# Layer 0 of a four-layer graph network: tie count, list sweeps and overflow rounds placed elsewhere between the two steps

## The chip, the cores and the metric

The kernel runs on one core of a Trainium2 chip. The metric is the device time of one execution in microseconds, the median of three runs. A profile of one more execution, recorded by the hardware, gives each instruction's start and duration. TensorE is called PE here, its weight loads PEld, VectorE DVE, ScalarE ACT, GpSimd POOL and SyncE SP. SP only issues transfers.

## The reference

There are 4096 nodes of 256 features and a sparse 4096 x 4096 adjacency matrix. Four layers follow each other, each as `x = x + layer(relu(layernorm(x)), adj)`. The change lies in layer 0, which takes two steps of a diffusion; its attention is cut to the largest probabilities that together reach 0.9:

```python
def _top_p_attention(X, W1, W2, W3):
    q = X @ W1.T @ W2.T
    k = X @ W3.T
    probs = softmax(q @ k.T)
    idx = argsort(-probs)
    sp = take_along_axis(probs, idx); cs = cumsum(sp)
    keep_sorted = cs - sp < 0.9
    A = probs * mask            # mask: keep_sorted put back in place
    return A / A.sum(-1, keepdims=True)

R = S + eye(N); R = R / R.sum(-1, keepdims=True)   # S: adj
Xf = Xa = X
for n in range(2):
    A = _top_p_attention(Xa, W1, W2, W3)
    Xf = R @ Xf
    Xa = A @ Xa
    Z = Z + Xf @ U1[n].T + Xa @ U2[n].T
return layernorm(X + Z) * ln_g + ln_b
```

Layers 1 to 3 are a graph convolution with tanh, a graph attention with four heads, and a convolution with relu. They stand after everything told here.

## The kernel before

The rows are worked in 32 blocks of 128 (`NB`), numbered 0 to 31. For each block, step n of layer 0 makes the row of logits (PE, `logits`, into PSUM pieces `pl`), its exponentials (ACT, `exps`, into a tile `e` of 128 x 4096), and looks for the threshold that keeps 0.9 of the sum. Nothing is sorted. The search is a ping-pong between two engines:

- ACT makes full or partial passes over `e`: `s0 r0` and `s1 r1` over 1024 columns, `s2 r2` and `s3` over all 4096 (a sign pass and a relu pass, line L1269). The number is the round.
- DVE turns their sums into the next guess by a dozen operations of one column each: `u0`, `u1`, `u2`, and at the end `bnd`, of some forty such operations.
- DVE then takes everything below the bound (`below`, L1475, a pass over 4096 columns into the tile `near`), the eight largest of each of 16 pieces (`seg`, L1483), merges them to a list of the largest (`lst`, L1495), decides the threshold (`dec`), and cuts the row (`cut`, L1535, another pass over 4096).

A row can have several values equal to the threshold. `ties_pe` (PE, L1558) counts such rows of a block by a product of one column, `ties` (ACT, L1564) copies the count to an integer, and `drop` (DVE, L1543) reads it into a register and branches: only if it isn't zero are the surplus equal values removed. Everything that reads the cut row comes after. In step 0 the count of a block is put into the last column of the PSUM bank in which the block before has its keys and queries (`keys_pe`, tag `pr`, one bank), so it must come after `keys_pe`.

After the cut, PE transposes the row in eight groups (`flip0` to `flip7`, L1604, into PSUM tiles of the tag `pmisc`, two banks), ACT copies each (`take`, L1610), and PE multiplies (`attend`, L1619). In step 0 the result is turned (`turn_pe`, `turn`, the copy `zt`), multiplied by weights (`xa_pe`, `h_pe`, copies `hu` by `copy_xa` and `store_h`, which go to the tables `heads_d`, `base_d`, `far_d`, `near_d`), and made to the keys and queries of step 1 (`keys_pe`, copied by `keys` as `kt` and `q`). The tag `pr` has one bank, so `keys_pe` waits until `hu` has been copied from it.

The order of PE, DVE and ACT is written out by hand. `ORDERS[n]` is a table of words, `name@offset`; `period(b)` goes through it and calls each word for block b + offset, so a period holds pieces of several blocks. A word is skipped if it was done ahead of its time. `LEADS[n]` is such a list before the first period of a step. In the last periods of step 0 (30 to 34) other pieces are put in by `inserts`: after the word named, the listed functions are called. They do three further things:

- `guessing(k)`: steps of `guess(1, ...)`, first estimates of the thresholds of step 1. For each of seven groups of 512 queries there is a product `py` (PE, L1040), a DVE operation (L1044) and four products (L1051), then a chain of 16 short DVE operations (L1063 to L1077). `last_queries` copies the queries of blocks 30 and 31 (ACT) into `near`, which the seventh group reads.
- `listing(k)`, and `L` in the lead: steps of `listed_columns`, which makes the lists of nonzero columns of the adjacency matrix. The step at `take1` of period 32 transposes `marks` (L787). 20 rounds of a MAX8 and a MATCH_REPLACE8 follow (L818, L819); the last three, the sweeps (`SWEEPS`), go over all 1024 keys. Then come a reduction (`fits`) and four copies of overflow lists by SP (L830), 8 overflow rounds of 32 rows (L840, L841), and two index tables, `column` and `adj_row`.
- `ahead1(b, words)`: words of step 1 for block b, done during step 0.

Step 1 mixes neighbours with the lists: POOL gathers rows by `column` and `adj_row` (L889, indirect DMAs, from `far_d` in the first half), PE multiplies them (L920, L921, tile `pr`). Each period of step 1 has two such mixes. POOL and SP are not under the written order: there the tile framework orders the instructions. [...] A PE product of float32 shows as two instructions in the profile.

Of the kernel before, what the change touches and what calls it, by code (L numbers as in the profile page):

```python
# [63 lines left out]
F32 = mybir.dt.float32  # L64
# [12 lines left out]
P = 128  # L77
N = 4096
D = 256
NB = N // P  # L80
# [585 lines left out]
def fast_layers(  # L666
# [85 lines left out]
    def marking(pool, marks):  # L752

        parts = []
        for k in range(NB * QUARTERS):
            while len(parts) < min(k + ADJ_BUFS, NB * QUARTERS):
                b, q = divmod(len(parts), QUARTERS)
                parts.append(pool.tile([P, CA, P], F32, name="adj"))
                nc.sync.dma_start(parts[-1], adjt[b, :, q * CA : (q + 1) * CA, :])
            b, q = divmod(k, QUARTERS)  # L760
            nc.vector.tensor_reduce(
                marks[:, :, q, b], parts[k], AX.X, ALU.max, apply_absolute_value=True
            )
            yield
# [165 lines left out]
    ps = layer0.enter_context(tc.tile_pool(name="ps", bufs=2, space=PSUM))  # L930
# [53 lines left out]
    def some(steps, k):  # L984

        for _ in zip(range(k), steps):
            pass
# [21 lines left out]
    def by_node(kt, r):  # L1009

        pt = ps.tile([P, 4, P], F32, name="pt", tag="pmisc")
        for k in range(4):
            nc.tensor.transpose(pt[:, k, :], kt[:, (4 * r + k) * P : (4 * r + k + 1) * P], ident)
        nc.scalar.copy(kn[:, :, :P], pt)

    def add_moments(r, pm, last):

        for k in range(4):
            nc.tensor.matmul(
                pm[:, : P + 1], kn[:, k, :P], kn[:, k, :], start=(r == 0 and k == 0), stop=(r == last and k == 3)  # L1020
            )
# [58 lines left out]
    def front(h0, kt, xs, marked, early):  # L1080
# [97 lines left out]
    G G M u2:0 s2:1 s3:0 M G G r2:1 logits0:2 exps0:2 M G G M bnd:0|u2:1  # L1178
    """,
        """  # L1180
    u2:0 logits1:1 s3:0 exps1:1 s0:1 r0:1 L4 bnd:0 below:0 L99 logits0:2 exps0:2 u0:1 s1:1 r1:1 logits1:2 exps1:2 u1:1 s2:1
    r2:1
    """,
    )

# [19 lines left out]
    def layer0_step(n, kt):  # L1205
# [344 lines left out]
        def ties_pe(b):  # L1550

            s = state[b]
            if n or b == 0:
                bank = ps1.tile([P, 512], F32, name="pties", tag="pr")
            else:
                bank = state[b - 1]["pkq_bank"]
            s["ties"] = bank[:1, 511:]
            nc.tensor.matmul(s["ties"], end["extra"][:, b : b + 1], ones, start=True, stop=True)  # L1558
# [472 lines left out]
    with ExitStack() as st:  # L2031
        s0 = st.enter_context(tc.tile_pool(name="s0", bufs=1))
        h0 = s0.tile([P, NB, D], F32, name="h0")
        kt0 = s0.tile([P, N // 2], F32, name="kt0")

        wu = []
        for i, u in enumerate((u1t, u2t)):
            wu.append(s0.tile([P, DC, 2, D], F32, name=f"wu{i}"))
            for n in range(2):
                nc.sync.dma_start(wu[i][:, :, 1 - n, :], u[n].rearrange("(c p) m -> p c m", p=P))  # L2040
        adj_pool = st.enter_context(tc.tile_pool(name="adj0", bufs=ADJ_BUFS))
        marked = marking(adj_pool, marks)
        period, verify, enter, early, lead, query = layer0_step(0, kt0)
        period1, verify1, enter1, early1, lead1, _ = layer0_step(1, kt1)

        def ahead(i, guesses):
            some(guesses, EARLY_GUESSES[i] if i < len(EARLY_GUESSES) else 0)
            for b, words in EARLY.get(i, ()):
                early(b, *words.split())

        with tc.tile_pool(name="front", bufs=1) as xs, tc.manual_schedule(engines=MANUAL):
            guesses = front(h0, kt0, xs, marked, ahead)
        own = st.enter_context(tc.tile_pool(name="own0", bufs=1))
        with tc.manual_schedule(engines=MANUAL):
            enter(h0, own, marked)
            lead(LEADS[0], M=marked, G=guesses)
            for b in range(NB - 2):
                period(b)
            some(marked, NB * QUARTERS)

            pm = ps.tile([P, 2, 512], F32, name="pl")
            first = adj_pool.tile([P, CA, P], F32, name="adj").rearrange("p l i -> p (l i)")[:, :512]
            nc.sync.dma_start(first, q_d[1][:, :512])
            lists = listed_columns(marks, e_pool.tile([P, N], F32, name="e"), ps)

            def sums_of(lo):
                if lo:
                    return ps1.tile([P, NB, 2], F32, name="pst", tag="pa")
                return pm[:, 1, : 2 * NB].rearrange("p (b k) -> p b k", k=2)

            guesses = guess(1, pm[:, 0], sums_of, first, SAMPLED[1] * P)

            def nodes(r):
                return lambda: by_node(kt1, r)

            def sums(r):
                return lambda: add_moments(r, pm[:, 0], SAMPLED[1] // 8 - 1)

            def listing(k):
                return lambda: some(lists, k)  # L2080

            def guessing(k):
                return lambda: some(guesses, k)

            def ahead1(b, words):
                return lambda: early1(b, *words.split())

            def queries():
                for g in range(4):
                    cols = slice(max(g * 1024, 512), min((g + 1) * 1024, (NB - 2) * P))  # L2090
                    nc.sync.dma_start(near[:, cols], q_d[1][:, cols])

            def last_queries():
                for b in range(NB - 2, NB):
                    nc.scalar.copy(near[:, b * P : (b + 1) * P], query(b))

            period(
                NB - 2,
                inserts={
                    "take1": [nodes(0)],  # L2100
                    "take2": [sums(0)],
                    "take3": [nodes(1)],
                    "take4": [sums(1)],
                    "take5": [nodes(2)],
                    "flip7": [sums(2), guessing(1)],
                    "take7": [guessing(1)],
                    "attended": [guessing(1)],
                },
            )
            period(  # L2110
                NB - 1,
                inserts={
                    "take1": [guessing(1)],
                    "attend7": [guessing(1), ahead1(0, "logits0")],
                    "turn": [ahead1(0, "exps0")],
                },
            )
            queries()
            period(
                NB,  # L2120
                inserts={
                    "take1": [listing(1), ahead1(0, "logits2 exps2")],
                    "take2": [listing(2), ahead1(0, "s0")],
                    "take3": [listing(3), ahead1(0, "r0")],
                    "take4": [listing(3), ahead1(0, "u0"), ahead1(1, "logits0")],
                    "take5": [listing(3), ahead1(0, "s1 r1")],
                    "take6": [listing(3)],
                    "take7": [listing(3), ahead1(0, "u1")],
                    "turn": [ahead1(1, "exps0 logits2 exps2")],
                },  # L2130
            )
            period(
                NB + 1,
                inserts={
                    "keys": [ahead1(0, "logits1 exps1 s2 r2"), guessing(3), listing(1)],
                    "xa_pe": [guessing(2), listing(1)],
                    "copy_xa": [last_queries],
                    "h_pe": [guessing(9), listing(2)],
                },
            )  # L2140
            period(NB + 2)
            lead1(LEADS[1], L=lists)
            verify()

    with ExitStack() as st:
        s1 = st.enter_context(tc.tile_pool(name="s1", bufs=1))
# [125 lines left out]
    with ExitStack() as st:  # L2272
# [3 lines left out]
        ps = st.enter_context(tc.tile_pool(name="gcnps", bufs=2, space=PSUM))  # L2276
# [76 lines left out]
    with ExitStack() as st:  # L2353
# [4 lines left out]
        ps = st.enter_context(tc.tile_pool(name="gatps", bufs=2, space=PSUM))  # L2358
# [153 lines left out]
    with ExitStack() as st:  # L2512
        adj_pool = st.enter_context(tc.tile_pool(name="lastadj", bufs=6))
        wk = st.enter_context(tc.tile_pool(name="lastwk", bufs=3))
        ps = st.enter_context(tc.tile_pool(name="lastps", bufs=2, space=PSUM))
# [15 lines left out]
@with_exitstack  # L2531
def graph_layers(ctx: ExitStack, tc: tile.TileContext, *given: bass.AP):
    nc = tc.nc
    dram = ctx.enter_context(tc.tile_pool(name="verdict", bufs=1, space=DRAM))
    wrong = dram.tile([1, 1], I32, name="wrong")
    fast_layers(tc, *given, wrong)
    again = nc.values_load(wrong[0:1, 0:1], min_val=0, max_val=2 * N + 2 * P)
    with tc.If(again != 0):
        general_layers(tc, *given)
# [54 lines left out]
```

## Time and profile before

| | |
|---|---|
| median of 3 runs | 2910.83 us (2905.03 to 2912.14) |
| the profiled execution | 2910.45 us, its span 2908.7 us |
| PE, DVE, ACT, POOL busy | 87%, 80%, 68%, 38% of the span |
| ACT full and partial passes (L1269), 320 in all | 859.5 us |
| step 1, 1200 to 1300 us: PE, DVE, ACT, POOL busy | 94.62, 88.65, 82.71, 66.55 us |

The page divides the span into 40 slices of 72.7 us, one digit for each, the busy share in tenths. A row of an engine's timeline gives start, duration (both in us), engine, line, operation, output and input, how often, and in brackets how long the engine had been idle before it and what ended that. A row "DVEq L1543" is the branch of `drop`. Step 0 ends and step 1 begins between about 1050 and 1190 us.

### The profile page before, as it was taken

To read this page: it belongs to the slowest core of one execution; us is meant where nothing else is said; L and a number is where in the kernel's file an instruction comes from. 1 tells how busy PE (TensorE), PEld (TensorE's weight loads), DVE (VectorE), ACT (ScalarE), POOL (GpSimd) and SP (SyncE) were. 2 spreads that over 40 slices of the span, in tenths; PEclk is the share of its full clock that TensorE was granted. 3 is DMA by queue.
4 is the path that set the end of the run, shared out by engine and by line. 5 is a ranking of instruction groups with operands and counts; after the bars stand their busy time and mean duration, and the time that the engine had idled before them with its cause. 6 is when DMAs were issued, how large, how long until landed. Compare 5 with 4: busy or idle time off the path is not lost. (4 is left out here: it accounts for less than half of the span.)

```text
span 2908.7 us, 43850 instructions
## 1 busy us (share of the span) xinstructions
PE 2523.0 (87%) x12359; PEld 1850.5 (64%) x12359; DVE 2312.7 (80%) x9516; ACT 1976.6 (68%) x3289; POOL 1098.0 (38%) x1152
## 2 busy tenths in 40 slices
PE   5769999999999884699999999999895776999777
PEld 4537777777777762467676766677773554788444
DVE  4799999999999866898989879999964765888200
ACT  2689999999999634887888878788520123999100
POOL 3200000000000001488888554344425752764476
PEclk7779999999999996899999999999996887999887
DMA  7611222222222113244444433334337653654576
GB/s 254 222 55 59 92 69 87 89 69 91 80 75 89 40 40 103 64 126 126 122 136 118 134 111 102 99 117 123 101 98 227 209 165 104 173 164 121 160 210 183
DMA packets 227371, 349.57 MB, mean 120 GB/s; under 512 B 34727, under 2 KB 160172, under 8 KB 227116
## 3 DMA queue, kind: packets, MB, share of 16 engines
q1 hardware_dynamic: 185820, 237.70, 25.7%
q0 software_dynamic: 40320, 108.72, 13.6%
q8 instruction: 101, 1.65, 0.2%
q14 instruction: 154, 1.26, 0.1%
q10 hardware_dynamic: 976, 0.23, 0.0%
HBM read 280.22 MB, written 66.28 MB: 119 GB/s over the span
## 5 line engine op out<-in xcount | busy, mean ns | idle before, releaser
L1269 ACT ACTIVATE unread<-e,next_pair 128x4096 uint8<-128x4096 f32 (+1 forms) x320 | 859.5, 2686 | 160.9 <-DVE next_pair L1365 109.0
L1619 PE MATMUL pa<-va,at 128*128 128x256 f32 x2048 | 495.2, 387 | 0.0
L1619 PE MATMUL pa<-h,at 128*128 128x256 f32 x2048 | 469.0, 379 | 0.1
L1619 PEld LDWEIGHTS pa<-va,at 128*128 128x128 f32 x2048 | 376.4, 193 | 65.4 <-issue 21.6
L1619 PEld LDWEIGHTS pa<-h,at 128*128 128x128 f32 x2048 | 376.6, 190 | 45.3 <-issue 0.5
L1483 DVE MAX8 best<-near 128x8 f32<-128x256 f32 x1024 | 394.6, 415 | 0.1
L1610 ACT COPY at<-pat 128x512 f32<-128x512 f32 x512 | 284.0, 577 | 135.3 <-PE pat L1604 135.1
L1236 PE MATMUL pl<-kt,qb 64*128 64x512 f32 x1024 | 280.4, 657 | 91.3 <-ACT e L1250 88.4
L1604 PE MATMUL pat<-ident,e 128*128 128x128 f32 x2048 | 305.0, 279 | 51.2 <-DVEq L1543 25.1
L1604 PEld LDWEIGHTS pat<-ident,e 128*128 128x128 f32 x2048 | 240.0, 142 | 139.1 <-DVEq L1543 47.8
L1485 POOL COPY eighth<-best 128x16 f32<-128x16 f32 x64 | 47.1, 736 | 722.7 <-DVE best L1483 711.7
L1250 ACT ACTIVATE e<-pl,minus_guess 128x1024 f32<-128x1024 f32 x256 | 284.3, 1125 | 26.8 <-PE pl L1236 26.7
L1475 DVE SCALAR_TENSOR_TENSOR near<-e,end_hi 128x4096 f32<-128x4096 f32 x64 | 286.6, 4477 | 0.1
L1535 DVE SCALAR_TENSOR_TENSOR e<-e,end_t 128x4096 f32<-128x4096 f32 x64 | 286.2, 4472 | 0.2 <-issue 0.2
L889 POOL DMA_INDIRECT vg<-v_d,column x256 | 243.4, 951 | 91.0 <-issue 67.7
L920 PE MATMUL acc<-vg,ac 128*128 128x256 f32 x640 | 215.9, 489 | 66.3 <-DMA vg<-v_d,column 29.6
L920 PEld LDWEIGHTS acc<-vg,ac 128*128 128x128 f32 x640 | 146.9, 247 | 132.1 <-issue 59.8
L1236 PEld LDWEIGHTS pl<-kt,qb 64*128 64x128 f32 x1024 | 89.8, 194 | 195.7 <-ACT e L1250 156.4
L889 POOL DMA_INDIRECT vg<-mixed_d,column x128 | 180.5, 1410 | 57.6 <-issue 32.4
L2407 PE MATMUL acc<-u,tabg 128*65 128x128 f32 x1280 | 170.2, 280 | 13.5 <-DVE u L2397 13.5
L889 POOL DMA_INDIRECT vg<-far_d,column x128 | 166.6, 1301 | 39.0 <-issue 38.1
L2394 ACT ACTIVATE u<-targets,tabg 128x128 f32<-128x128 f32 x544 | 162.1, 389 | 10.0 <-DMA targets_x<-steep_d 10.0
(608 smaller groups left out, 4427.7 us busy)
## 6 DMA issues: line engine op xcount, KB each, us to landing
adj<-in_adjt SPq DMA_DIRECT2D x128, 512.0 KB
ac<-adjc_d SPq DMA_DIRECT2D x64, 320.0 KB
adjc_d<-ac SPq DMA_DIRECT2D x32, 320.0 KB
vg<-v_d SPq DMA_DIRECT2D x64, 128.0 KB
targets<-steep_d SPq DMA_DIRECT2D x32, 256.0 KB
ac<-adjc_d SPq DMA_DIRECT2D x32, 256.0 KB
table_d<-tab SPq DMA_DIRECT2D x32, 132.0 KB
tabg<-table_d SPq DMA_DIRECT2D x32, 132.0 KB
```

The costliest lines, as they stand in the source:

```text
L889: nc.gpsimd.indirect_dma_start(out, None, rows, bass.IndirectOffsetOnAxis(ap=index, axis=0))
L920: nc.tensor.matmul(acc, ac[:, k, :], v[:, k, :], start=(k == 0), stop=False)
L1236: nc.tensor.matmul(pl[:, r, :], s["qb"][rows], kt[rows, j * 512 : (j + 1) * 512], start=True, stop=True,)
L1250: nc.scalar.activation(s["e"][:, j * 1024 : (j + 1) * 1024], pl.rearrange("p r c -> p (r c)"), AF.Exp, bias=minus_guess[:, b : b + 1], acc ...
L1269: nc.scalar.activation(unread[:, :width], s["e"][:, :width], func, bias=s["at"], scale=-1.0, accum_out=s["signs"] if func == AF.Sign else ...
L1475: nc.vector.scalar_tensor_tensor(near, s["e"], end["hi"][:, b : b + 1], s["e"], op0=ALU.is_lt, op1=ALU.mult, accum_out=s["low"])
L1483: nc.vector.max(best[:, k, :], near[:, k * (N // SEG) : (k + 1) * (N // SEG)])
L1535: nc.vector.scalar_tensor_tensor(s["e"], s["e"], last, s["e"], op0=ALU.is_ge, op1=ALU.mult, accum_out=s["held"])
L1604: nc.tensor.transpose(pt[:, k, :], s["e"][:, c * P : (c + 1) * P], ident)
L1610: nc.scalar.copy(at, s["pt", g])
L1619: nc.tensor.matmul(s["pa"], s["at", g][:, k, :], va[:, c, :D], start=(c == 0), stop=(c == NB - 1))
L2407: nc.tensor.matmul(s["acc"][:, h, :], s["tab"][:, k, h * (DK + 1) : (h + 1) * (DK + 1)], s["u"][:, k, h, :], start=(k == 0), stop=False,)
```

## The change

It has three parts, all of them of place and order.

- The tie count of block 31 (`NB - 1`) gets a bank of the tag `pmisc`. `ties_pe` and `ties` are done at the end of period 31, after `turn`; `drop`, `flip0` and `flip1` follow `cut` at once in period 32, before `store_h` and `keys_pe`.
- The four steps of `listing` in period 33 (three sweeps, and what follows them up to the SP copies) move into period 32, after `attended` and after `turn`.
- `u2` and `s3` of block 0 of step 1 move from the lead into period 33, after `copy_xa` and ahead of `last_queries`. In the lead, the rest of the lists goes from ahead of `logits0:2` to behind `u1:1`, in two pieces: eight steps there, the rest after `r2:1`.

```diff
@@ LEADS[1]
-    u2:0 logits1:1 s3:0 exps1:1 s0:1 r0:1 L4 bnd:0 below:0 L99 logits0:2 exps0:2 u0:1 s1:1 r1:1 logits1:2 exps1:2 u1:1 s2:1
-    r2:1
+    logits1:1 exps1:1 s0:1 r0:1 logits0:2 exps0:2 bnd:0 u0:1 below:0 s1:1 r1:1 logits1:2 exps1:2 u1:1 L8 s2:1 r2:1 L9
@@ ties_pe
             if n or b == 0:
                 bank = ps1.tile([P, 512], F32, name="pties", tag="pr")
+            elif b == NB - 1:
+                bank = ps.tile([P, 512], F32, name="pties", tag="pmisc")
             else:
                 bank = state[b - 1]["pkq_bank"]
@@ the end of step 0
+            def ahead0(words):
+                return lambda: early(NB - 1, *words.split())
+
@@ period(NB - 1)
-                    "turn": [ahead1(0, "exps0")],
+                    "turn": [ahead0("ties_pe ties"), ahead1(0, "exps0")],
@@ period(NB)
+                    "cut": [ahead0("drop flip0 flip1")],
                     "take1": [listing(1), ahead1(0, "logits2 exps2")],
...
-                    "turn": [ahead1(1, "exps0 logits2 exps2")],
+                    "attended": [listing(2)],
+                    "turn": [ahead1(1, "exps0 logits2 exps2"), listing(2)],
@@ period(NB + 1)
-                    "keys": [ahead1(0, "logits1 exps1 s2 r2"), guessing(3), listing(1)],
-                    "xa_pe": [guessing(2), listing(1)],
-                    "copy_xa": [last_queries],
-                    "h_pe": [guessing(9), listing(2)],
+                    "keys": [ahead1(0, "logits1 exps1 s2 r2"), guessing(3)],
+                    "xa_pe": [guessing(2)],
+                    "copy_xa": [ahead1(0, "u2 s3"), last_queries],
+                    "h_pe": [guessing(9)],
```

In the engines' instruction orders the same instructions stand in both kernels. On SP the four copies L830 come ahead of the store of `far_d` for block 30 instead of among the loads of `va` (the operand of step 1's products, read from `heads_d`); on POOL one branch comes ahead of three iotas.

## The prediction

> **What bounds the kernel now.** I read the page's slices first, then the busy time by stage, then each engine's timeline over the seam between the two steps of layer 0, about 1050 to 1190 us. Both steps keep TensorE (PE) over 90% busy; the seam does not.
>
> ```profile
> PE   5769999999999884699999999999895776999777
> 1050.00:1090.00 40.00, 34.06 (x152) 24.10 (x150) 20.30 (x86) 16.06 (x31) 0.10 (x1) 0.87 0.05 15
> 1120.00:1160.00 40.00, 11.02 (x27) 3.83 (x27) 30.69 (x145) 17.37 (x21) 8.18 (x9) 0.54 0.43 130
> 1160.00:1190.00 30.00, 3.90 (x10) 1.22 (x10) 20.76 (x117) 25.76 (x28) 19.83 (x23) 0.52 0.32 81
> ```
>
> The columns after the length are PE, weight loads, VectorE (DVE), ScalarE (ACT), POOL, then clock, DMA share, GB/s. From 1120 to 1190 PE works 15 us of 70: it waits for the first blocks' threshold search, a ping-pong of DVE and ACT. That search is the path. Its stops:
>
> ```profile
> 1060.44 0.16 DVE L773 MEMSET marks<- 128x8 f32 x4 [10.31 <-DVEq L1543]
> 1100.15 1.61 DVE L1044 SCALAR_TENSOR_TENSOR near<-py,mean,near 128x512 f32<-128x512 f32 x2 [13.54 <-PE py L1040]
> 1119.19 1.22 DVE L818 MAX8 e<-e 128x8 f32<-128x1024 f32 x1
> ...
> 1126.15 3.71 ACT L1269 ACTIVATE unread<-e,next_pair 128x4096 uint8<-128x4096 f32 x1 [12.50 <-DVE next_pair L1365]
> ...
> 1137.74 4.48 DVE L1475 SCALAR_TENSOR_TENSOR near<-e,end_hi 128x4096 f32<-128x4096 f32 x1
> ...
> 1156.88 3.70 ACT L1269 ACTIVATE unread<-e,next_pair 128x4096 uint8<-128x4096 f32 x1
> ...
> 1145.93 0.60 PE L853 MATMUL pt<-e 32*128 32x16 f32 x2 [21.41 <-DVE e L848]
> ...
> 1190.78 1.10 PE L1604 MATMUL pat<-ident,e 128*128 128x128 f32 x8 [2.24 <-DVEq L1543]
> ```
>
> Block 31's cut ends at 1050.1 and its flips start at 1060.4, because its tie count stands behind keys_pe. DVE then has a 13.5 us hole, yet its last sweep of the lists comes after it and holds ACT's s3:0 for 12.5 us. Then L99 (8 us, 1142.15 to 1150.14) precedes u0:1, so block 1's full pass s2:1 starts at 1156.88. Step 1's first flip follows at 1190.78.
>
> **The change part by part.** Sums are against the profiled execution: 2910.45 us, span 2908.7 plus 1.75. The median, 2910.83, is 0.4 above.
>
> *Ties ahead.* ties_pe moves to just after turn_pe (ends 1053.19), ACT's tied copy (0.14) after zt (ends 1053.82). In the row above, flips start 1.0 us after the tied copy's end, so flip0 moves from 1060.4 to about 1054.9. Only part arrives. ACT's take0 remains queued behind hu, kt and q, and keys_pe stays tied to hu (1056.6), now behind eight transposes. Cold (keys 2.2 us as traced) take0 is at 1059.7 and the marks transposes at 1060.3, against 1062.2: gain 2.0. Warm (keys 1.2, marks 1.0, the next four logits 0.8 less) gain 4.9. The Trainium skill ("TensorE: Matmul & The Clock Gate", Part 1: The HAM clock gate) halves the clock after an idle window of about 3.4 us. The old gap (3.36 us) gave 0.50; the new gaps, 1.7 and 1.2, would by that rule stay warm: 4.9. But gaps of 1.17 and 1.61 before 1026.7 were followed by a granted 0.57 in 1028 to 1032, which argues for 2.0. I take 3. PE is 4.00 busy in every 4 us from 1064 to 1088, so this arrives whole at the end of period 32.
>
> *Sweeps into the hole.* Four listing steps move: three sweeps at 1.22+0.09+1.21 with small gaps, 2.56 each, and the tail (fits 1.22, memsets 0.35, 0.30, 0.33): 9.9 us. They now follow u1:0, from 1083.6 to 1093.5; the next DVE work waits for py at 1097.1. Cover 3.6 us, so cost 0; without it, up to 9.9. Of the old places, two lay under the PE work of xa_pe and h_pe (worth 0); the third plus tail (1119.19 to 1123.99) frees 4.8. The four list copies on SP (2.53 us of issue) move from the middle of the va loads to ahead of the far_d store of block 30, which they hold to about 1096. What queues behind (q_d, a qb, heads_d) is next wanted by logits0:2 at about 1120. Worth 0. On POOL only a branch passes three iotas.
>
> *u2:0 and s3:0 to copy_xa.* u2:0 (2.16 us, as from 1123.90) follows the sixth L1044, at 1108.1, ending 1110.3; s3:0 runs to 1114.2 instead of 1130.0. Its price: behind s3:0 on ACT stand the two query copies (0.5) that the seventh py needs, so py moves from 1112.8 to 1114.7 after a PE gap of 4.8 us. By the same rule that gap ends cold; the trace's cold rows are about twice the warm ones, so guess ends its products 1.0 (0 to 1.9) later still: 1118.6 against 1115.78, its chain of 3.5 at 1122.1 against 1119.3. The hu copy behind goes out at 1115, a far_d row first gathered after 1147: nothing.
>
> *Overflow rounds behind the first pass.* Now bnd:0 starts at 1122.1 (was 1131.5), 6.25 long: 1128.4; u0:1 2.0: 1130.4, its s0 and r0 done by 1124.3 since PE no longer stands at L852/L853; below:0 4.5: 1134.9 while s1 and r1 run; u1:1 2.0; s2:1 at 1137.0. That is 19.9 ahead of 1156.88.
>
> *Given back.* The rest of the lists now lies between u1:1 and the end of u2:1: 0.4, eight rounds 5.5, 2.2 to the table, 1.5 to column, then 5.0 woven with u2:1 and verify: u2:1 ends 1151.5, where its r2:1 would allow 1146.2. So s3:1 starts 1151.6 against 1167.08: **15.5 ahead**. From there DVE and ACT have the old order; flip0 of block 0 comes at about 1175.3.
>
> *Does it reach the end?* In step 1 PE is 94.6 of 100 busy, and the mixes come every 29.5 us with no wait ahead of them. The gathers are the danger: column comes only 1.9 us sooner, so 18 gathers at 1.25 end at 1170, and 29 at 1184. PE wants the first mix at 1201.4, so that slack falls from about 46 to 31 us.
>
> ```profile
> 1149.38 1.11 POOL L889 DMA_INDIRECT vgx<-far_d,column  x1 [52.40 <-DVE e L869]
> ...
> 1216.89 2.34 PE L920 MATMUL pr<-vg,ac 128*128 128x257 f32 x10
> ...
> 1362.32 4.47 DVE L1535 SCALAR_TENSOR_TENSOR e<-e,end_t 128x4096 f32<-128x4096 f32 x1
> ...
> 1363.33 4.28 POOL L889 DMA_INDIRECT vg<-far_d,column  x1 [0.30 <-issue]
> ```
>
> A gather that meets a DVE pass took 4.28 us, not 0.95. The first batch met none; now it meets cut(0) and below(1). The Trainium skill ("SBUF — State Buffer", SBUF: two separate sides) speaks against the change: whoever starts first holds the shared port for its whole instruction. By the trace two meetings cost 6.7 us, by the rule up to 9.0. Either way the 29 end by 1193, of which the last eleven serve mixes at 1231 and later. Cost 0 by both.
>
> Sum: +3 (ties) +16.9 (search) −4.4 (lists) = 15.5; 2910.45 − 15.5 = **2895**, as a median too. With 2.0 or 4.9 for the first term, cold or warm py, and 1 us of weaving, 12 to 20: 2890 to 2899.
>
> **Rivals.** *Gain mostly not passed on (a part at most):* s3:0 waiting longer, the DVE sweeps reaching past py, or the take0 queue eating the ties. For it: four engines in order, each re-timed. Against: 3.6 us of cover. Time 2899 to 2905.
>
> *It doesn't do what it says:* gathers set the first mixes, so PE starts early and waits there; only their 1.9 us remain: 2909. Against: 31 us of slack.
>
> *Slower, by one mechanism:* in step 1's first half POOL has no idle left. Its cycle starts at 30.8 us with two blocked gathers, has one of 34.2 at 1311 to 1346, then locks at 29.5, lagging the mixes by 10.6 (1375.26 against 1364.65). If the new phase left it at 34.2, it would lose 4.7 us a period against PE. The cycle begun at 1219.5 ends at 1249.4 and serves a mix at 1276.0, 26 us later; used up in six of sixteen periods, that leaves ten times 4.7 on PE, less 15.5: 2942. It decides above 31.1 us a cycle (29.5 plus 26 over 16). Against: the blocked time shrinks when POOL falls behind, as the lock shows, and the phase of the passes to the mixes is set by the unchanged order.
>
> **How the numbers follow.** This kernel's measurement can tell 0.3% (8.7 us) from no change; the line is 2902.1. Forecast (2890 to 2899) 0.66; more than that (to 2884) 0.05; partly lost (2899 to 2905) 0.14, of which 0.09 is still beyond 0.3%; no gain 0.07; slower 0.08. Faster 0.80, same 0.12, slower 0.08. The range 2886 to 2905 leaves out no gain, slower, and a little at the fast end.
>
> **What would show it.** Right: flip0 of block 31 near 1055; sweeps ended before py; s3:0 near 1110; s2:1 near 1137; s3:1 near 1151.6; first mix near 1201 with no wait; all later stages shifted alike. Wrong: marks still at 1062; py(7) past 1118; a DMA wait ahead of L920 in the first periods; a POOL cycle above 31.1 us.

## The result, and the profile after

The kernel after takes 2894.2 us (median of 4 runs, 2889.9 to 2895.7) against 2911.05 for the kernel before (4 runs). The ratio is 0.9944, with a 95% interval of 0.9926 to 0.9962. That is 16.8 us less, outside the 0.3% that the measurement can tell from no change. Predicted were 2895 and 15.5 us less. The profiled execution spans 2893.8 us.

Its page's slices of TensorE (PE), and the stages by window (length, then PE, weight loads, VectorE, ScalarE, GpSimd, clock, DMA share, GB/s):

```profile
PE   5769999999999895799999989999985776999777
1120.00:1160.00 40.00, 14.05 (x36) 5.38 (x36) 32.41 (x182) 26.80 (x32) 8.50 (x9) 0.54 0.38 116
1160.00:1190.00 30.00, 16.70 (x70) 10.81 (x71) 26.90 (x127) 25.01 (x29) 24.21 (x20) 0.69 0.26 66
```

PE does 30.8 us of work between 1120 and 1190 where it did 15, because step 1's attention now begins inside that stretch. The timeline of the kernel after has these stops (start, duration, instruction, and in brackets the idle time ahead and what ended it). The line numbers moved by one: L1269 is now L1268, and behind the tie count L1604 is now L1605.

```profile
1055.10 0.59 ACT L1641 COPY zt<-pt 128x512 f32<-128x512 f32 x1 [3.79 <-PE pt L1636]
...
1056.82 1.06 PE L1605 MATMUL pat<-ident,e 128*128 128x128 f32 x8 [1.63 <-ACT e L1249]
...
1061.17 1.97 PE L787 MATMUL pt<-ident,marks 128*128 128x128 f32 x8 [1.13 <-ACT at L1611]
...
1098.26 1.61 DVE L1044 SCALAR_TENSOR_TENSOR near<-py,mean,near 128x512 f32<-128x512 f32 x2 [2.32 <-PE py L1040]
...
1111.53 3.71 ACT L1268 ACTIVATE unread<-e,next_pair 128x4096 uint8<-128x4096 f32 x1 [4.98 <-DVE next_pair L1364]
...
1115.23 0.48 ACT L2099 COPY near<-q 128x128 f32<-128x128 f32 x2
...
1115.77 2.08 PE L1040 MATMUL py<-near,mk 128*128 128x512 f32 x2 [4.67 <-ACT near L2099]
...
1138.99 3.71 ACT L1268 ACTIVATE unread<-e,next_pair 128x4096 uint8<-128x4096 f32 x1 [1.59 <-DVE next_pair L1364]
...
1142.82 3.71 ACT L1268 ACTIVATE unread<-e,next_pair 128x4096 uint8<-128x4096 f32 x1
...
1151.45 3.71 ACT L1268 ACTIVATE unread<-e,next_pair 128x4096 uint8<-128x4096 f32 x1 [2.28 <-DVE skip L1280]
...
1160.23 3.71 ACT L1268 ACTIVATE unread<-e,next_pair 128x4096 uint8<-128x4096 f32 x1 [2.43 <-DVE steep L1348]
...
1175.14 2.99 PE L1605 MATMUL pat<-ident,e 128*128 128x128 f32 x12 [2.23 <-DVEq L1542]
```

They are the copy `zt` of block 31, its first flips (1056.82), the marks (1061.17), the first L1044 behind the sweeps (1098.26), s3:0 (1111.53), the two query copies behind it (1115.23), the seventh py (1115.77), s2:1 and r2:1 (1138.99, 1142.82), s3:1 (1151.45), the next block's first full pass (1160.23) and the first flip of step 1's block 0 (1175.14, before 1190.78).

Two executions are not in step when they reach this seam. The copy `zt` of block 31 starts at 1055.10 here and at 1053.23 before, and over all profiles of this document it lies between 1047.0 and 1055.1. The same transposes one block earlier (block 30) lie between 1017.5 and 1023.4; most of this difference was already there at 210 us. From there to block 31's transposes it takes 28.9, 30.6 or 32.3 us (30.6 and 32.3 in two profiles of the kernel after). So I measure each profile by **S**, the stretch from the start of that copy to block 0's first flip: 137.6 us before, 120.0 after. (The expectations below call this point the end of the copy; their figures for S, too, count from its start.) Three rows of the kernel before, for comparison, are its `zt`, its marks and its s3:1:

```profile
1053.23 0.59 ACT L1640 COPY zt<-pt 128x512 f32<-128x512 f32 x1 [3.79 <-PE pt L1635]
...
1062.21 1.97 PE L787 MATMUL pt<-ident,marks 128*128 128x128 f32 x8
...
1167.08 3.71 ACT L1269 ACTIVATE unread<-e,next_pair 128x4096 uint8<-128x4096 f32 x1
```

The seam is 17.5 us shorter, and the product at L1837 (L1836 before) that starts at 2107.18 before starts at 2090.01 after: nothing is lost again in step 1. (The two profiled executions end 14.9 us apart; the 2.3 us between are lost in the layers behind, for a reason that I did not follow.) "Aligned" below means less 1.87, the difference between the two starts of `zt`.

### The profile page after: what moved, and what is told of

Its sections match the earlier page's. It is cut to its first block, busy times and chain, and to the rows that moved or that the text cites. A ratio compares the mean times of both kernels' runs of the same rounds, so it can differ in the third digit from the quotient of the medians.

```text
span 2893.8 us, 43853 instructions
## 1 busy us (share of the span) xinstructions
PE 2529.9 (87%) x12359; PEld 1856.8 (64%) x12359; DVE 2311.4 (80%) x9516; ACT 1975.2 (68%) x3289; POOL 1104.3 (38%) x1152
## 5 line engine op out<-in xcount | busy, mean ns | idle before, releaser
L1268 ACT ACTIVATE unread<-e,next_pair 128x4096 uint8<-128x4096 f32 (+1 forms) x320 | 859.6, 2686 | 160.4 <-DVE next_pair L1364 109.0
L1605 PE MATMUL pat<-ident,e 128*128 128x128 f32 x2048 | 305.0, 279 | 51.1 <-DVEq L1542 23.6
L1605 PEld LDWEIGHTS pat<-ident,e 128*128 128x128 f32 x2048 | 239.9, 142 | 138.9 <-DVEq L1542 46.3
L1484 POOL COPY eighth<-best 128x16 f32<-128x16 f32 x64 | 30.1, 470 | 702.1 <-DVE best L1482 691.5
L1249 ACT ACTIVATE e<-pl,minus_guess 128x1024 f32<-128x1024 f32 x256 | 284.1, 1124 | 17.7 <-PE pl L1235 17.5
```

Source lines behind the costliest of these rows:

```text
L1249: nc.scalar.activation(s["e"][:, j * 1024 : (j + 1) * 1024], pl.rearrange("p r c -> p (r c)"), AF.Exp, bias=minus_guess[:, b : b + 1], acc ...
L1268: nc.scalar.activation(unread[:, :width], s["e"][:, :width], func, bias=s["at"], scale=-1.0, accum_out=s["signs"] if func == AF.Sign else ...
L1605: nc.tensor.transpose(pt[:, k, :], s["e"][:, c * P : (c + 1) * P], ident)
```

## The experiments

All ratios are to runs of the kernel before on the same chip. The ratio is the estimate from all runs of a kernel, so it need not be exactly the quotient of the two medians. S comes from one profile each. The runs fell on several chips. On two of them (R and T) every kernel run there took 7 to 8% longer than elsewhere, and only the stretch ahead of the gathers can be compared directly with the rest (last section).

| kernel | chip | median, us | before there | ratio (95%) | S, us |
|---|---|---|---|---|---|
| after | – | 2894.2 | 2911.05 | 0.9944 (0.9926–0.9962) | 120.0 |
| ties back | Q | 2895.5 | 2909.5 | 0.9955 (0.9941–0.9970) | 123.7 |
| sweeps back | Q | 2898.9 | 2909.5 | 0.9966 (0.9956–0.9976) | 128.4 |
| u2 and s3 back | Q | 2890.7 | 2909.5 | 0.9935 (0.9919–0.9951) | 119.9 |
| rounds back | Q | 2906.2 | 2909.5 | 0.9985 (0.9977–0.9992) | 132.9 |
| queries first | R | 3115.0 | 3130.2 | 0.9945 (0.9932–0.9959) | 135.6 |
| rounds later | R | 3122.6 | 3130.2 | 0.9981 (0.9967–0.9996) | 146.5 |
| both | R | 3114.6 | 3130.2 | 0.9939 (0.9923–0.9955) | 139.1 |
| rounds late | R | 3115.3 | 3130.2 | 0.9954 (0.9941–0.9967) | 125.1 |
| queries first | T | 3119.6 | 3139.4 | 0.9943 (0.9923–0.9963) | 137.5 |
| both | T | 3126.8 | 3139.4 | 0.9960 (0.9949–0.9970) | 140.1 |
| after, again | U | 2891.2 | 2906.5 | 0.9940 (0.9925–0.9956) | 120.4 |
| **queries first** | U | **2884.9** | 2906.5 | **0.9922** (0.9906–0.9938) | **114.2** |

**Ties back.**

```diff
-            elif b == NB - 1:
-                bank = ps.tile([P, 512], F32, name="pties", tag="pmisc")
-                    "turn": [ahead0("ties_pe ties"), ahead1(0, "exps0")],
+                    "turn": [ahead1(0, "exps0")],
-                    "cut": [ahead0("drop flip0 flip1")],
```

> The ties part alone undone: the last block's ties are again summed in the keys' bank inside its own period, the rest of the change stays. Measured by S, the stretch from the end of the last block's zt copy to the first flip of step 1's block 0: 137.6 us before, 120.0 after. Theory: the marks come 2.9 us later and all behind them is a chain without slack, so S is about 123 and the time about 2897 (a ratio to before of 0.9954). Rival (the marks' delay is swallowed, because the lead's boundary waits for the tail of the guesses and the lists, not for the marks): S stays at 120 to 121 and the time at 2894.

The timeline of this kernel:

```profile
1058.70 1.97 PE L1603 MATMUL pat<-ident,e 128*128 128x128 f32 x8 [1.63 <-DVEq L1542]
1060.55 1.94 PE L787 MATMUL pt<-ident,marks 128*128 128x128 f32 x8
```

The marks (second row) come 8.7 us after the copy instead of 6.1 (5.6 in the repeat), and S is 3.3 to 3.7 longer than in the two profiles of the kernel after. The theory holds, the rival (nothing) falls. The ratios point the same way, but their intervals overlap, so S carries this reading.

**Sweeps back.**

```diff
-                    "attended": [listing(2)],
-                    "turn": [ahead1(1, "exps0 logits2 exps2"), listing(2)],
+                    "turn": [ahead1(1, "exps0 logits2 exps2")],
-                    "keys": [ahead1(0, "logits1 exps1 s2 r2"), guessing(3)],
-                    "xa_pe": [guessing(2)],
+                    "keys": [ahead1(0, "logits1 exps1 s2 r2"), guessing(3), listing(1)],
+                    "xa_pe": [guessing(2), listing(1)],
-                    "h_pe": [guessing(9)],
+                    "h_pe": [guessing(9), listing(2)],
```

> The sweeps' part alone undone: the four listing steps are again in the period behind the last block (one each at the keys and the transposed keys, two at the end), the rest stays. Theory: VectorE's hole of about 13 us while the last block attends is empty again, and the third sweep with the tail of the lists, about 4.8 us, lies between the last guess and the lead's boundary: S about 124.8, time about 2899 (ratio 0.9960). Rival A (the lists' work was beside other work all the time): S 120 to 121, 2894 to 2895. Rival B (the page of lists coming later also delays block 0's recall by its DMA loads): S above 128, over 2903.

S rose by 8.3, not 4.8 (by the ratios 6 to 8 us are lost). VectorE's timeline shows where:

```profile
1105.94 0.75 DVE L1044 SCALAR_TENSOR_TENSOR near<-py,mean,near 128x512 f32<-128x512 f32 x1 [1.00 <-PE py L1040]
1106.61 1.22 DVE L818 MAX8 e<-e 128x8 f32<-128x1024 f32 x1
...
1111.14 0.16 DVE L1364 SCALAR_TENSOR_TENSOR next_pair<-den,next_pair 128x1 f32<-128x1 f32 x1
...
1117.75 0.75 DVE L1044 SCALAR_TENSOR_TENSOR near<-py,mean,near 128x512 f32<-128x512 f32 x1 [6.45 <-PE py L1040]
...
1124.36 1.22 DVE L818 MAX8 e<-e 128x8 f32<-128x1024 f32 x1
...
1126.93 1.22 DVE L821 TENSOR_REDUCE fits<-e 128x1 f32<-128x1024 f32 x1
```

The third sweep and the tail (from 1124.36 to 1129.14) are the 4.8 of the theory. The second sweep (1106.61 to 1109.15) now stands ahead of u2:0, which this kernel, unlike the kernel before, has at that place: it holds s3:0, and with it the query copies and the last guess, another 2.5 us. The rest, 1.0, is the sixth L1044, which itself came 1.1 later after the copy than in the kernel after. This is not the edit's doing alone: the first four py instructions ahead of it took 2.75 us here and 1.98 in that one profile of the kernel after, but 2.83 in its repeat and 2.7 to 3.8 in all others. Rival B's number was met by another mechanism: the gathers were not involved, since s2:1, ahead of the first gather, is already 8.3 us later after the copy (92.2 against 83.9).

**u2 and s3 back.**

```diff
-                    "copy_xa": [ahead1(0, "u2 s3"), last_queries],
+                    "copy_xa": [last_queries],
-    logits1:1 exps1:1 s0:1 r0:1 logits0:2 ...
+    u2:0 logits1:1 s3:0 exps1:1 s0:1 r0:1 logits0:2 ...
```

> The move of u2 and s3 alone undone: u2 of block 0 and its similarities are back at the head of the lead, behind the last guess, and the query copies stand alone at their word. Theory: the move was worth almost nothing, because holding the query copies for s3:0 delayed py(7) and with it the last guess by about 5 us, as much as u2 and s3 cost in the lead (2.1 and 3.8): S 119 to 121, time 2893 to 2895. Rival (the move is worth what it takes out of the lead, 5.9): S about 126, time about 2900 (ratio 0.9962).

S is 119.9 and the ratio 0.9935: the theory holds, this part of the change brings nothing where the others are in place. (The median, 2890.7, lies below the expected 2893 to 2895; the interval of the ratio covers that of the kernel after.) The timelines of PE (first row) and ScalarE (second) show the exchange:

```profile
1108.91 1.02 PE L1040 MATMUL py<-near,mk 128*128 128x512 f32 x2
...
1117.53 3.71 ACT L1268 ACTIVATE unread<-e,next_pair 128x4096 uint8<-128x4096 f32 x1 [7.79 <-DVE next_pair L1364]
```

The seventh py comes 57.0 us after the copy instead of 60.7, is warm (1.02 us instead of 2.08), and the last L1044 is 4.8 us earlier. In return s3:0 starts 9.2 us later (65.6 against 56.4) and ends inside the lead.

**Rounds back.**

```diff
-    ... s0:1 r0:1 logits0:2 exps0:2 bnd:0 u0:1 below:0 s1:1 r1:1 logits1:2 exps1:2 u1:1 L8 s2:1 r2:1 L9
+    ... s0:1 r0:1 L4 bnd:0 below:0 L99 logits0:2 exps0:2 u0:1 s1:1 r1:1 logits1:2 exps1:2 u1:1 s2:1 r2:1
```

> The rounds' part alone undone: the overflow lists are again ahead of the lead's boundary (first four) and between below:0 and logits0:2 (the rest), instead of behind u1:1 and r2:1. Theory: the lists again stand in front of block 0's first pass. s2:1 comes about 13 us later and nothing is given back behind it, so of the 16.8 us gained some 6 to 7 remain: S about 129 to 131, time about 2904 (ratio 0.9976). Rival (the place of the lists decides nothing since VectorE has to do them in the lead in either place): S 120 to 122, 2894 to 2896.

S is 132.9, 12.7 more than in the kernel after and somewhat more than the theory's 9 to 11; by the ratios 12 to 13 us are lost. PE's timeline has the old wait again (5.46 us for the same row in the kernel after):

```profile
1140.77 0.60 PE L853 MATMUL pt<-e 32*128 32x16 f32 x2 [18.30 <-DVE e L848]
```

This is the largest part. The rival, that VectorE must do the lists in either place, falls: ahead of `bnd:0` and `u0:1` they hold ScalarE's passes; behind `u1:1` most of them run while ScalarE makes s2:1 and r2:1.

The four parts undone one by one add to 3.5, 8.1, −0.3 and 12.7, 24 us in all (each against the mean S of the two profiles of the kernel after). The whole change moves S by 17.3. They are not independent: each undoing is measured in the presence of the others.

**Queries first.** The rows of the kernel after point at a better order. In "u2 and s3 back" the move costs as much as it gains, and the price is that the query copies stand behind s3:0 on ScalarE.

```diff
-                    "copy_xa": [ahead1(0, "u2 s3"), last_queries],
+                    "copy_xa": [last_queries, ahead1(0, "u2 s3")],
```

> One swap in the kernel after: at the word copy_xa the query copies of the last block come first and u2 and s3 of step 1's block 0 second. Theory (s3:0 ahead of the copies holds py(7) and the chain of the last guess): the guess ends about 5 us earlier, s3:0 is done beside it, the lead's boundary starts 5 us earlier: S about 115, time about 2889 (ratio 0.9925). Rival (the copies were not the holder, or s3:0 then ends too late for the boundary): S 119 to 121, time 2893 to 2895.

> The same swap again (query copies first at copy_xa, u2 and s3 second), for its time on another chip: the first trial met a chip on which the kernel before itself took 3130 us, and on which small VectorE instructions stood 1.1 to 3.8 us apart while GpSimd issued the gathers. Up to these gathers that trial kept to the theory: exps of block 1 began 5.9 us earlier than in the kernel after. Theory: on a chip where the kernel before takes about 2910 the 5 to 6 us stay to the first flip: S about 114.5, time about 2889, ratio 0.9925. Rival (the gathers, now 6 us earlier, lie in another place beside the boundary's small instructions and cost there what the swap gains): S 119 to 121, 2893 to 2895.

> The kernel after, unchanged, on the same chip as the query swap beside it. Theory: on a chip where the kernel before takes about 2910 it repeats: S 120, ratio 0.9944. On a chip where the kernel before takes about 3130 (as in four trials so far) the gathers lie beside the boundary's small instructions and stretch them as they did with the swap: S about 138 to 142, ratio 0.995 to 0.997. Rival (its gathers miss the boundary because they start 6 us later than with the swap): S about 126 there and a ratio below 0.994.

> The swap (query copies first at copy_xa), on the same chip as the kernel after unchanged. Theory on a chip where the kernel before takes about 2910: S about 114.5, about 5 us faster than the kernel after, ratio 0.9925. Theory on a chip where it takes about 3130: S 135.6 to 137.5 as in the two trials so far, and 3 to 6 us under the kernel after there. Rival (the gathers' place eats the swap's gain): same time as the kernel after within 1.5 us, and S within 1.5 of it.

On chip U, beside the kernel after: 2884.9 against 2891.2 us, S 114.2 against 120.4. The gain of 6 is that of the theory, and this kernel beats both. The timeline of the kernel on chip U:

```profile
1099.65 0.50 ACT L2099 COPY near<-q 128x128 f32<-128x128 f32 x2
...
1104.19 1.02 PE L1040 MATMUL py<-near,mk 128*128 128x512 f32 x2
1105.05 3.71 ACT L1268 ACTIVATE unread<-e,next_pair 128x4096 uint8<-128x4096 f32 x1 [4.90 <-DVE next_pair L1364]
...
1137.56 3.71 ACT L1268 ACTIVATE unread<-e,next_pair 128x4096 uint8<-128x4096 f32 x1 [2.27 <-DVE skip L1280]
...
1161.26 1.10 PE L1605 MATMUL pat<-ident,e 128*128 128x128 f32 x8 [2.24 <-DVEq L1542]
```

The seventh py now runs while s3:0 starts: the copies, done before it, no longer hold py. s3:1 begins 90.5 us after the copy of block 31 instead of 96.4, and the lead of 5.8 stays to the flip. On R and T the same 5.9 and 5.8 are there at s3:1, but then the small VectorE instructions behind it, block 0's list merges and those of `bnd:1` between them, are stretched (last section), S is 135.6 and 137.5, and the ratio is 0.9945 and 0.9943.

**Rounds later, and both.**

```diff
-    ... u1:1 L8 s2:1 r2:1 L9
+    ... u1:1 L8 s2:1 r2:1
-                period1(b)
+                period1(b, inserts={"exps1": [listing(99)]} if b == -1 else {})
```

> The kernel after with the last lists moved on from behind r2:1 to block 1's own period, behind exps1, ahead of the last similarities. Theory: the 2.3 us given back at s3:1 come back, since the gathers have about 31 us of slack before the mixes and start some 5 to 10 us later: S about 117.7, time about 2892. Rival A (the lists only move the delay to the similarities behind them): S 119 to 121, 2893 to 2896. Rival B (the later gathers collide with block 0's own gathers on the queue and the mixes wait): S falls, the time does not: 2896 or more, with a wait of TensorE for the queue at the mixes.

> Both edits, the query copies first and the last lists in block 1's period. Theory: the two are on different stretches of one chain and add: S about 113, time about 2887 (ratio 0.992). Rival (the second loses its effect when the lead starts earlier, because the lists then do not stand in front of anything late): S about 115, time as with the copies first alone, 2889.

> Both edits again, query copies first and the last lists in block 1's period, on another chip. Theory: beside the 5.9 us of the first, the 2.3 us given back at s3:1 are regained: S about 112, time about 2887, ratio 0.992. Rival (as the first trial hints, where the gathers and the lists came later and the boundary's small instructions ended 3.5 us later than with the swap alone: the lists then stand in front of block 0's boundary instead of block 1's similarities): S 118 to 123, 2893 to 2898.

ScalarE's timeline of "both" on chip T has r2:1, s3:1 and the next block's first full pass, as the rows of the kernel after above:

```profile
1132.71 3.71 ACT L1268 ACTIVATE unread<-e,next_pair 128x4096 uint8<-128x4096 f32 x1
...
1139.23 3.71 ACT L1268 ACTIVATE unread<-e,next_pair 128x4096 uint8<-128x4096 f32 x1 [0.17 <-DVE next_pair L1364]
...
1151.42 3.71 ACT L1268 ACTIVATE unread<-e,next_pair 128x4096 uint8<-128x4096 f32 x1 [2.49 <-DVE steep L1348]
```

From r2:1 to s3:1 it takes 6.5 instead of 8.6 us, so the 2.1 us are regained, as expected. But from s3:1 to the next pass it takes 12.2 instead of 8.8: the lists stand in front of that pass and lose 3.4. "Rounds later" shows the same two stretches, 6.5 and 12.2. The theory's step was right and its sum wrong; rival A, that the delay only moves to the pass behind, describes what the rows show, though S itself (146.5 and 139.1 to 140.1 on these chips) can't test its figure. For the times of "both", the two chips do not agree on a difference from "queries first" (0.9939 against 0.9945 on R, 0.9960 against 0.9943 on T, all intervals overlapping).

**Rounds late.**

```diff
-    ... u1:1 L8 s2:1 r2:1 L9
+    ... u1:1 L8 s2:1 r2:1
-                period1(b)
+                period1(b, inserts={"stood": [listing(99)]} if b == 0 else {})
```

> The kernel after with the last lists moved much further, into block 0's own period behind its first standing sums: a trial of how much slack the gathers have. Theory: the gathers of the overflow rounds start some 25 to 40 us later than in the kernel after, use up the about 31 us between their batch and the mixes that need it, and the lists now stand in the recall of block 0: S stays near 117 to 118, but TensorE waits at the first mixes and the time is 2900 to 2912. Rival (slack is larger, since the mixes of the overflow rows come late in the period): time 2890 to 2895.

The gathers started 19 us later after the copy (113.3 against 94.0). S is only 125.1 on chip R because here the gathers begin at 1162.74, so the stretching that comes with them there (last section) falls mostly behind the first flip. PE's first mix came at 1217.86, long after the batch's last gather (1205.64), and with no wait ahead of it: VectorE's list merges behind the first flip had themselves waited 2.2 to 2.6 us each (marked "remote"), and PE came late. So the run says nothing on how far the slack reaches; that stays open. What it adds: s3:1 and the next pass come at the undisturbed distances (6.5 and 8.8), but from s3:1 to the last step of block 0's threshold (L1525) it takes 23.3 us against 18.3, with its merges no further apart than in the kernel after (1163.50 to 1166.36). Behind r2:1 the lists cost 2.1, behind exps1 3.4, behind `stood` 5.0: the place in the change was the cheapest of the three tried. (The last two figures are from chips R and T, set against the kernel after elsewhere.)

## Why the prediction was right, step by step

- **Ties ahead**, 3 (2.0 to 4.9). Aligned, the flips start at 1054.95 (predicted 1054.9) and the marks at 1059.3, 2.9 us earlier. The disputed clock came out between the two readings. Windows of 3 us of the kernel after (the granted clock is the number ahead of the DMA share):

```profile
1054.00:1057.00 3.00, 1.37 (x10) 0.80 (x9) 0.15 (x4) 1.90 (x5) 0.00 (x0) 1.00 0.00 0
1057.00:1060.00 3.00, 2.45 (x16) 1.96 (x14) 0.00 (x0) 1.38 (x3) 0.00 (x0) 0.83 0.20 69
1060.00:1063.00 3.00, 1.87 (x9) 1.57 (x8) 0.60 (x1) 1.50 (x4) 0.10 (x1) 0.50 0.13 40
```

  The clock was still 1.00 when the flips began (eight took 1.06 us), averaged 0.83 over the next window, so `keys` took its products warm in part, and fell to 0.50 for the marks (eight took 1.97 us). By the rule of the Trainium skill ("TensorE: Matmul & The Clock Gate", Part 1: The HAM clock gate), as the prediction read it, gaps of 1.63, 0.55 and 1.13 us, each far below its idle window, would have left it warm and given 4.9. The trace's counterexample was the better guide. Between 1054.6 and 1058.4 PE did only transposes and a product of one column; whether the clock counts these as work, no run here shows. That the value between the two was right is partly luck: over the twelve profiles that keep this part the marks come 5.6 to 6.5 us after the start of `zt` (9.0 before), which is a gain of 2.4 to 3.4, and 2.4 to 2.6 in ten of them.
- **Sweeps into the hole**, cost 0. Aligned they start at 1084.1, VectorE is free before py, and its wait there shrank from 13.54 to 2.32 us. The statement that two of the old places were "worth 0" holds for the old order alone: with u2:0 in period 33 one of them would have cost 2.5 more.
- **u2:0 and s3:0 to copy_xa.** Aligned s3:0 starts at 1109.7 (predicted about 1110.4), py at 1113.9 (1114.7) and cold (2.08 us), as argued, and the guess ends at 1122.7 (1122.1). The prediction saw the price and put the later guess in its sum. What it did not say is that price and gain cancel: with the move undone the last L1044 is 4.8 us earlier and the whole no slower (S 119.9).
- **Rounds behind the first pass.** s2:1 at 1137.1 aligned, predicted 1137.0; "rounds back" shows this as the largest term.
- **Given back**, 4.4: the term that was mis-sized. Aligned, s3:1 starts at 1149.6, not 1151.6, so 2.3 of the 19.8 us that s2:1 gained are given back. The index tables were in time (`column` done at 1146.2 aligned, predicted 1146.6), but the part from there to the end of u2:1, in which the lists' operations alternate with the search's, took 3.2 us where I had put 5.0. "Both" confirms the size: without lists there, the stretch from r2:1 to s3:1 is 2.1 us shorter.
- **Does it reach the end?** Yes. The first mix is at 1201.28 without a wait, 29.8 us after the end of the 18th gather (1171.49; predicted 31). Two gathers of the first batch met VectorE's passes, as predicted, and took 4.05 and 4.17 us, 6.3 more together than two that met none (0.95); the prediction had 6.7 by the trace and up to 9.0 by the rule that it cites. Both ended 0.8 us after the pass that they met (1175.02 and 1182.01). The batch ended at 1191.6 (predicted before 1193). GpSimd's next batch waited for PE, not the reverse:

```profile
1171.79 4.05 POOL L889 DMA_INDIRECT ac<-in_adjt,adj_row  x1 [0.30 <-issue]
...
1178.65 4.17 POOL L889 DMA_INDIRECT ac<-in_adjt,adj_row  x1 [0.30 <-issue]
...
1203.89 0.97 POOL L889 DMA_INDIRECT ac<-in_adjt,adj_row  x1 [7.60 <-PE pr L920]
```

- **Rivals.** None came. The loss to a GpSimd cycle that outlasts PE's period is excluded for the kernel after: no mix of the first half of step 1 waits for a gather, and they come every 29.5 us.

The sum was 15.5; 2.1 too much was taken off for the lists, which makes 17.6, and the seam measures 17.5. The medians say 16.8; single runs of either kernel scatter over 6 to 7 us. The parts were right in their sum and in their stops; what each is worth alone is another matter, as the undoings show: 24 us in all, and nothing for one of them.

## What to carry to other kernels

When a step is moved ahead of another on an engine whose order is written out, look at what now stands behind it there and who waits for that: here two copies, half a microsecond together, behind a pass of 3.7 us ate the whole gain of a move, and swapping the two words was worth 6 us. Work that must be done on the bounding engine was cheapest directly behind the instruction that starts a long pass on its partner; there some 11 us of mostly list work (1138.81 to 1149.92) cost the search 2.1 to 2.3. Measure a local change from a mark just ahead of it, since here executions of the same kernel were up to several microseconds apart long before the place of the edit.

## What the runs showed of the hardware

On chips R and T the kernel before takes 3130 and 3139 us, against 2906.5 to 2911 elsewhere. "Queries first" has a profile from each of R, T and U; those from R and U span 3094.8 and 2883.1 us. Up to the gathers they don't differ: `zt` starts at 1047.6 and 1047.0. At the seam S is 21.4 us longer on R, and in the first half of step 1 the mixes come every 38.5 us there instead of 29.6. These are VectorE's merges of a list on chip R ("queries first") and, last three rows, in the kernel after:

```profile
1154.05 0.29 DVE L1494 MAX8 tops<-best 128x8 f32<-128x128 f32 x1 [2.69 <-remote]
...
1162.47 0.29 DVE L1494 MAX8 tops<-rest 128x8 f32<-128x128 f32 x1 [3.77 <-remote]
...
1175.08 0.29 DVE L1494 MAX8 tops<-rest 128x8 f32<-128x128 f32 x1 [3.02 <-remote]
```

```profile
1164.64 0.29 DVE L1494 MAX8 tops<-best 128x8 f32<-128x128 f32 x1
...
1165.45 0.29 DVE L1494 MAX8 tops<-rest 128x8 f32<-128x128 f32 x1
...
1167.61 0.29 DVE L1494 MAX8 tops<-rest 128x8 f32<-128x128 f32 x1
```

The instructions last equally long, but from the first merge to the fifth it takes 21.0 us on chip R and 3.0 us in the kernel after, while GpSimd issues the same gathers every 1.25 us in both. "Remote" means that the trace doesn't show what was waited for. On R the stretching began some 15 us or more after the first gather of a burst (1135.69), not at once, and ended after the last (1170.94). What it is that waits, the runs don't settle, nor whether the gathers cause it: they go with it in time, and the same kernel on chip U has the same gathers without it. It doesn't hit every kernel alike, since S on R lies between 125.1 (gathers last) and 146.5. So a ratio from R or T contains this loss beside what the edit does, and it hides what an edit does behind the gathers.
